# Selective scan: sums issued ahead of the fill of their turn, and the projection's matmuls moved into the turns with sums

## The chip, the cores and the metric

One core of a Trainium2 chip runs the whole program. The metric is device time in microseconds (us) of one execution. Engines: PE (TensorE, matmuls), DVE (VectorE), ACT (ScalarE), POOL (GpSimd), SP (SyncE, which issues the DMAs here). Each works through its own queue in order, and they meet at semaphores.

## The reference, cut to what matters

The model has two layers on four images of 64 x 64 tokens with 128 channels: attention and a recurrent network, then a selective scan in four directions and a mixture of experts. The change lies in the selective scan of the second layer:

```python
x_dbl = einsum('bkdl,kcd->bkcl', xs, x_proj_w)          # x projection: dt's rank 8, B 16, C 16
dts_r, Bs, Cs = x_dbl[:, :, :R], x_dbl[:, :, R:R+N], x_dbl[:, :, R+N:]
dt = softplus(einsum('bkrl,kdr->bkdl', dts_r, dt_proj_w) + dt_proj_b)
A = -exp(A_logs)
def step(h, inp):                                         # over the L = 4096 tokens
    dt_l, u_l, B_l, C_l = inp
    h = h * exp(dt_l[..., None] * A) + (dt_l * u_l)[..., None] * B_l[:, :, None, :]
    return h, einsum('bkdn,bkn->bkd', h, C_l)
ys = ys + Ds * xs                                         # and the four directions are added up
```

There are 4 images, K = 4 directions, 256 channels and N = 16 states for each channel, all in float32.

## The kernel before, in words

The function `scans` (from line 966) handles one direction k after the other, in the order 2, 3, 0, 1. A direction is cut into 33 **windows** of W = 500 tokens (4 blocks of 125), so there are 132 windows. A window has 16 **tiles**: for four states at a time (q = 0 to 3) and each of the four blocks. A tile holds 128 partitions x (2 channel halves x 4 states x 127 columns) = 1016 columns. Tiles of two neighbouring groups q alternate.

The order of all work is written by hand (`tc.manual_schedule()`): a loop over **turns** p issues the instructions of each turn to the engines' queues. A window takes 16 turns, and from here on turns are counted modulo 16, so that "turn 8" is p = 8, 24, 40 and so on. In the kernel before, the order of a turn p is:

- `finished(p)`: once a window, at turn 9, ACT copies the finished `y` from PSUM (L1337), and SP stores it.
- `at[p+1].fill()`: PE fills one of the two `db` PSUM buffers of the tile of turn p+1, with 8 small matmuls (L1241) for dt*u*B. The buffer was read by the scan of turn p-1. Beside each pair a matmul of zeros (L1250) adds nothing to `y`. This is called **F(p+1)** below.
- `at[p-1].carry()`: ACT copies the last states of the tile of turn p-1 into the decays of a later tile (L1286).
- `at[p].scan()`: DVE runs the scan (L1265), called **scan(p)**, which needs F(p) and its decays.
- `sums(p)`: at every even turn, 16 matmuls on 64 x 64 corners of the array (named by L1316 in the profile) add products of a group into `y`: **S(p)**. At turn 7, `add_other` (L1327, **add**) adds what an earlier direction left, or the skip term; not for k = 3.
- `at[p].times_c()`: POOL multiplies the states by C into `products` (L1299), a ring of 12 tiles. It may overwrite a place only when the sums have read it.
- `at[p+5].load()` (SP loads C rows), `before(p)` (SP loads `other`), `decay(p)` (ACT exponentials, L1206).
- `projections(p)`: the generator `project` prepares a later window in steps. `yield t` means: go on at turn t, counted from the window's own start, so -33 falls on turn 15 of the windows under way, and -15 on turn 1.

The steps of `project` that the text speaks of, all sharing the two PSUM banks of one tile, `mm = ps.tile([P, ND, CH], ...)`, made once:

- two x matmuls (L1110), **x1** and **x2**, into `mm[:, 0]`, and the ACT copy `xd` (L1115) out of it;
- the dt matmuls (L1129), **dt**, into both banks, then on ACT `e`, `low`, a logarithm back into `mm`, on POOL a product into `low` (L1145);
- two DVE maxima (L1154), **dt0** and **dt1**, which read bank 0 and bank 1 of `mm` at turns 13 and 14;
- POOL's `dtu` (L1157); the small transposes of B (L1162), **b_ps**, into `mm[:, 1]`; two DVE products `b_diag` (L1168) that read them at turns 2 and 3;
- ACT copies `quarters` (L1177), eight transposes (L1189), **T**, into both banks of `mm`, and the ACT copy `dtu_t` (L1191).

Of the kernel before, what the change touches and what calls it, by code (L numbers as in the profile page):

```python
# [965 lines left out]
def scans(ctx, tc, a, us, ys, flag):  # L966
# [19 lines left out]
    TILES = Q * NB  # L986
# [100 lines left out]
    def quartered(of, to, turned):  # L1087

        for half in range(2) if turned else (None,):
            i = NB if half is None else NB // 2  # L1090
            yield (
                to if half is None else to[:, :, 2 * half : 2 * half + 2],
                bass.AP(
                    of.tensor,
                    of.offset + (0 if half is None else (2 - 2 * half) * T),
                    [of.ap[0], [STEP, NS], [T, i], [1, 32]],
                ),
            )

    def project(v):  # L1100

        k = v.k
        yield -BEFORE
        v.u = work.tile([P, ND, W], F32, tag="u", name="u")
        for b, of, to in v.pieces:
            nc.sync.dma_start(v.u[:, :, to], us[b][k % 2][:, :, of])
        x_ps = mm[:, 0]
        for h, turn in enumerate((-33, -31)):
            yield turn
            nc.tensor.matmul(  # L1110
                x_ps[:, :W], w_x[:, h, k, :], v.u[:, h, :], start=h == 0, stop=h == ND - 1
            )
        yield -30
        xd = work.tile([P, W], F32, tag="xd", name="xd", bufs=1)
        nc.scalar.activation(xd, x_ps[:, :W], AF.Identity, bias=one)  # L1115
        v.c_rows = dram.tile([NB, N, T], F32, tag="c", name="c_rows")
        nc.sync.dma_start(
            v.c_rows.rearrange("i n t -> n i t"),
            xd[64 : 64 + N].rearrange("n (i t) -> n i t", i=NB),
        )  # L1120
        yield -29
        b_rows = work.tile([32 + N, NS, NB, 32], F32, tag="b_rows", name="b_rows", bufs=1)
        for to, of in quartered(xd[32 : 32 + N], b_rows[32:], False):
            nc.scalar.copy(to, of)
        yield -23
        pts = mm[:, :, :W]
        for h, row in enumerate(DT_ROWS):
            rows = slice(row, row + R + 1)
            nc.tensor.matmul(pts[:, h], w_dt[rows, k, :], xd[rows], start=True, stop=True)  # L1129
        yield -22  # L1130
        e = work.tile([P, ND, W], F32, tag="e", name="e", bufs=1)
        if v is todo[0]:

            nc.scalar.preload_act_table_set("natural_log_exp_and_others")
        if flag is None:
            nc.scalar.activation(e, pts, AF.Relu, scale=-1.0, bias=most)
            nc.scalar.activation(e, e, AF.Exp, scale=-1.0, bias=most)
        else:
            nth = todo.index(v)
            nc.scalar.activation(e, pts, AF.Exp, accum_out=largest[:, nth : nth + 1])  # L1140
        low = work.tile([P, ND * NS * P], F32, tag="low", name="low", bufs=1)
        bound = low[:, : ND * W].rearrange("p (h t) -> p h t", h=ND)
        nc.scalar.activation(bound, e, AF.Copy, scale=-0.5, bias=1.0)
        yield -21
        nc.gpsimd.tensor_mul(bound, bound, e)  # L1145
        if flag is None:
            for h in range(ND):
                nc.vector.tensor_max(bound[:, h], pts[:, h], bound[:, h])
        nc.scalar.activation(pts, e, AF.Ln, bias=1.0)
        yield -19  # L1150
        v.dt = work.tile([P, ND, W], F32, tag="dt", name="dt")
        for h, turn in enumerate((-19, -18)):
            yield turn
            nc.vector.tensor_max(v.dt[:, h], pts[:, h], bound[:, h])  # L1154
        yield -17
        dtu = work.tile([P, ND, W], F32, tag="e", name="dtu", bufs=1)
        nc.gpsimd.tensor_mul(dtu, v.dt, v.u)  # L1157
        yield -15
        b_ps = mm[:, 1, : NS * N].rearrange("p (s n) -> p s n", s=NS)
        for i in range(NS):  # L1160
            part = b_rows[32 : 32 + N, i].rearrange("n i t -> n (i t)")
            nc.tensor.transpose(b_ps[:, i, :], part, ident[32 : 32 + N, 32 : 32 + N])  # L1162
        yield -14
        v.b_diag = work.tile([P, NS, N, 32], F32, tag="b_diag", name="b_diag")
        quarters = work.tile([P, ND, NS, NB, 32], F32, tag="low", name="quarters", bufs=1)
        for turn, i in ((-14, 0), (-13, 2)):
            yield turn
            nc.vector.tensor_mul(  # L1168
                v.b_diag[:, i : i + 2].rearrange("p s n t -> p (s n) t"),
                b_ps[:, i : i + 2]  # L1170
                .rearrange("p s (n o) -> p (s n) o", o=1)
                .to_broadcast([P, 2 * N, 32]),
                ident32.rearrange("p (o t) -> p o t", o=1).to_broadcast([P, 2 * N, 32]),
            )
            h = i // 2
            for to, of in quartered(dtu[:, h], quarters[:, h], h):
                nc.scalar.copy(to, of)  # L1177
        yield -12
        v.b_other = work.tile([P, NS, N, 32], F32, tag="b_other", name="b_other")
        for r in range(2):  # L1180
            to, of = (slice(HALF * x, HALF * x + HALF) for x in (r, 1 - r))
            nc.sync.dma_start(v.b_other[to], v.b_diag[of])
        yield -11
        v.dtu = work.tile([P, ND, NS, P], F32, tag="dtu_t", name="dtu_t")
        turned = mm.rearrange("p h (s d) -> p h s d", s=NS)
        for h in range(ND):
            for i in range(NS):
                part = quarters[:, h, i].rearrange("p i t -> p (i t)")
                nc.tensor.transpose(turned[:, h, i, :], part, ident)  # L1189
        yield -10  # L1190
        nc.scalar.copy(v.dtu, turned)  # L1191
# [111 lines left out]
    def sum_of(pair, n):  # L1303

        v, q = pair[0].v, pair[0].q
        if q == 0 and n == 0:
            v.y = ps.tile([P, 2, CH], F32, tag="y", name="y", bufs=1)
            summed.append(v.y)
        for r in range(2):
            rows = slice(HALF * r, HALF * r + HALF)  # L1310
            for h, g in enumerate(pair):
                y = v.y[HALF * h : HALF * h + HALF, r, :W]
                begins = q == 0 and n == 0
                ends = q == Q - 1 and n == 3
                of, to = window_of(products, rows, g, n, v.data.start, y)
                nc.tensor.matmul(to, ident[rows, rows], of, start=begins, stop=ends)  # L1316
        if n == 3:
            summed.append(v.y if q < Q - 1 else None)

    def add_other(v):  # L1320

        if v.k == 3:
            return
        for r in range(2):
            rows = slice(HALF * r, HALF * r + HALF)
            for h in range(ND):
                nc.tensor.matmul(  # L1327
                    v.y[HALF * h : HALF * h + HALF, r, :W],
                    skips[rows, h, :] if v.back else ident[rows, rows],
                    v.other[rows, h, :],  # L1330
                    start=False,
                    stop=False,
                )
# [22 lines left out]
    with tc.manual_schedule():  # L1356
# [58 lines left out]
        def sums(p):  # L1415

            g, turn = divmod(p - 10, NB)
            for g, n in ((g, 0), (g, 1)) if turn == 0 else ((g, 2), (g, 3)) if turn == 2 else ():
                if g in range(len(pairs)):
                    sum_of(pairs[g], n)  # L1420
            w, turn = divmod(p - 23, TILES)
            if turn == 0 and w in range(len(todo)):
                add_other(todo[w])

        def finished(p):
            w, turn = divmod(p - 25, TILES)
            if turn == 0 and w in range(len(todo)):
                finish(todo[w])

        for p in range(-BEFORE, max(at) + 12):  # L1430
            finished(p)
            if p + 1 in at:
                at[p + 1].fill()
            if p - 1 in at:
                at[p - 1].carry()
            if p in at:
                at[p].scan()
            sums(p)
            if p in at:
                at[p].times_c()  # L1440
            if p + 5 in at:
                at[p + 5].load()
            before(p)
            decay(p)
            projections(p)
# [380 lines left out]
```

## Time and profile before

| | |
|---|---|
| median of 3 runs | 9569.09 us (9560.02 to 9577.49) |
| profiled execution | 9570.26 us, span 9568.5 us |
| scans, turns in full flow | about 3640 to 8905 us of the span |
| scan on DVE (L1265) | 2112 times, 2256 ns each |
| products on POOL (L1299) | 2112 times, 2149 ns each |
| matmuls of F (L1241) | 33792, 270 ns median, several at a time on strips of the array |
| matmuls of S (L1316) | 16896, 577 ns median, several at a time on corners of the array |

The span is what the hardware profiler recorded from the first to the last instruction; the execution's own time is a little longer. In an answer of the timeline a row has its start, its length (of several instructions run together where it says x2 and so on), the engine, the line, the tiles and shapes, and in brackets how long the engine had been idle before it and what ended that. Busy time by stage gives stretch, length and busy us (count) for PE, PE's weight loads, DVE, ACT and POOL, then PE's granted clock, the DMA share and GB/s.

### The profile page before, as it was taken

The page shows a single profiled execution, that of the slowest core. Times are in us where ns is not written, and L with a number is a line of the kernel's source. Part 1 is how long each engine was busy: PE and PEld are TensorE (multiplying, and loading weights), DVE is VectorE, ACT ScalarE, POOL GpSimd, SP SyncE. Part 2 cuts the span into 40 slices and gives each one's busy share as a digit, 9 for nine tenths or more (in the row PEclk, how much of TensorE's full clock was granted, in tenths as well). Part 3 has the DMA queues.
Part 4 walks back from the last instruction along what each step waited for, and adds up shares of the span by engine and source line. Part 5 has one row for each costly group of instructions (what it writes and reads, how often), then busy time and mean ns, then how long its engine had stood idle before and what let it go on. Part 6 is the DMA issues. An engine that isn't in the chain of part 4 may idle for free. (4 is left out here: it accounts for less than half of the span.)

```text
span 9568.5 us, 222640 instructions
## 1 busy us (share of the span) xinstructions
PE 8704.4 (91%) x94770; PEld 4134.2 (43%) x94770; DVE 8357.7 (87%) x5099; ACT 6855.5 (72%) x10362; POOL 5157.0 (54%) x2433
## 2 busy tenths in 40 slices
PE   7999999999989887999999999999999999999766
PEld 3222222222223334555555555555555555555223
DVE  6899999999978317999999999999999999999764
ACT  3888888888856456777778788877777777777321
POOL 0000000000001017999999999999999999999100
PEclk8999999999999898999999999999999999999887
DMA  4000000000011335666666666666666666666634
GB/s 174 27 8 36 8 8 34 8 8 8 10 51 53 115 122 155 170 171 170 170 168 160 163 160 160 161 167 170 170 171 171 170 170 171 170 170 164 225 119 181
DMA packets 530898, 1163.76 MB, mean 122 GB/s; under 512 B 76818, under 2 KB 444506, under 8 KB 502106
## 3 DMA queue, kind: packets, MB, share of 16 engines
q1 hardware_dynamic: 529882, 1149.30, 41.4%
q8 instruction: 748, 12.26, 0.5%
q14 instruction: 268, 2.20, 0.1%
HBM read 828.51 MB, written 182.15 MB: 106 GB/s over the span
## 5 line engine op out<-in xcount | busy, mean ns | idle before, releaser
L1265 DVE TENSOR_TENSOR_SCAN states<-decays,db 128x1016 f32<-128x1016 f32 x2112 | 4668.8, 2256 | 100.8 <-ACT decays L1286 60.9
L1299 POOL TENSOR_TENSOR products<-states,c_ring 128x1000 f32<-128x1000 f32 x2112 | 4456.2, 2149 | 219.4 <-PE y L1316 185.3
L1206 ACT ACTIVATE decays<-dt,a_logs 128x500 f32<-128x500 f32 x4224 | 3017.6, 714 | 90.4 <-DVE states L1265 4.3
L1241 PEld LDWEIGHTS db<-b_diag,dtu_t 32*128 32x128 f32 x16896 | 2050.9, 187 | 1607.1 <-DVE states L1265 1187.3
L1241 PE MATMUL db<-b_diag,dtu_t 32*128 32x128 f32 x16896 | 2429.4, 283 | 315.2 <-DVE states L1265 309.5
L1241 PE MATMUL db<-b_other,dtu_t 32*128 32x128 f32 x16896 | 2458.3, 284 | 0.0
L1250 PE MATMUL y<-zeros 32*128 32x128 f32 x14720 | 2122.0, 283 | 0.0
L1241 PEld LDWEIGHTS db<-b_other,dtu_t 32*128 32x128 f32 x16896 | 2049.7, 186 | 0.2 <-issue 0.2
L1316 PE MATMUL y<-products,ident 64*64 64x500 f32 x16896 | 2019.7, 592 | 1.2 <-POOL products L1299 1.2
L334 DVE TENSOR_TENSOR total<-total,ring 128x2048 f32<-128x2048 f32 x768 | 1759.1, 2291 | 67.7 <-DVE total L334 2.7
L1250 PEld LDWEIGHTS y<-zeros 32*128 32x128 f32 x14720 | 1771.8, 186 | 0.0
masks.py:197 POOL MEMSET ident<- 128x128 f32 x6 | 1.2, 204 | 2974.3 <-SPq L180 2677.7
L302 ACT ACTIVATE ring<-sa 128x2048 f32<-128x2048 f32 x640 | 1203.9, 1881 | 454.2 <-PE sa L287 454.2
L311 PE MATMUL av<-ring,v_at 128*32 128x512 f32 x8192 | 1010.0, 599 | 0.1
L1316 PEld LDWEIGHTS y<-products,ident 64*64 64x64 f32 x16896 | 541.2, 132 | 696.7 <-issue 568.1
L287 PE MATMUL sa<-q_at,k_at 32*128 32x512 f32 x5120 | 731.8, 641 | 63.3 <-ACT ring L302 41.6
L1286 ACT COPY decays<-states 128x8 f32<-128x8 f32 x2048 | 405.2, 198 | 535.7 <-DVE states L1265 519.4
L302 ACT ACTIVATE ring<-sb 128x1536 f32<-128x1536 f32 x512 | 741.2, 1448 | 0.4 <-PE sb L287 0.4
L287 PE MATMUL sb<-q_at,k_at 32*128 32x512 f32 x3072 | 555.7, 615 | 50.9 <-ACT ring L302 50.9
L311 PEld LDWEIGHTS av<-ring,v_at 128*32 128x32 f32 x8192 | 210.4, 109 | 701.2 <-issue 676.6
L287 PEld LDWEIGHTS sa<-q_at,k_at 32*128 32x128 f32 x5120 | 200.3, 183 | 618.5 <-ACT ring L302 310.2
L330 DVE TENSOR_TENSOR total<-ring 128x2048 f32<-128x2048 f32 x128 | 293.2, 2290 | 141.4 <-ACT ring L302 141.4
(210 smaller groups left out, 7962.9 us busy)
## 6 DMA issues: line engine op xcount, KB each, us to landing
c_ring<-c_rows SPq DMA_DIRECT2D x2112, 250.0 KB, 4.6
b_other<-b_diag SPq DMA_DIRECT2D x264, 512.0 KB, 6.5
weights<-in_w SPq DMA_DIRECT2D x32, 1024.0 KB, 12.8
u<-u_r SPq DMA_DIRECT2D x60, 500.0 KB, 5.7
y_r<-sum SPq DMA_DIRECT2D x60, 500.0 KB, 4.3
u<-u_c SPq DMA_DIRECT2D x60, 500.0 KB, 5.7
y_c<-sum SPq DMA_DIRECT2D x60, 500.0 KB, 4.1
x<-x SPq DMA_DIRECT2D x96, 256.0 KB, 2.6
```

The costliest lines, as they stand in the source:

```text
L287: nc.tensor.matmul(s[:, m, :], k[rows, tokens(t)], q[rows, chunk(chunk_state["c"])], start=True, stop=True,)
L302: nc.scalar.activation(ring[:, lo : lo + n, :], s[:, at : at + n, :], AF.Exp)
L311: nc.tensor.matmul(chunk_state["av"][rows, :], chunk_state["v"][:, t, rows], ring[:, at + i, :], start=t == 0, stop=t == NJ - 1,)
L330: nc.vector.tensor_add(total, chunk_state["first"], w)
L334: nc.vector.tensor_add(total, total, w)
L1206: nc.scalar.activation(to, dt, AF.Exp, scale=scale)
L1241: nc.tensor.matmul(bank.rearrange("p (n t) -> p n t", n=4)[:, :, to : to + 32], v.dtu[rows, h, s, :], b[rows, s, 4 * self.q : 4 * self.q + ...
L1250: nc.tensor.matmul(y[:, idle // 2, :P], zeros[rows], zeros[rows], start=False, stop=False)
L1265: nc.vector.tensor_tensor_scan(order(self.slot(states)), order(self.slot(decays, shift)), order(self.db[:, SKIP + shift :][:, : 2 * LANE]) ...
L1286: nc.scalar.copy(self.edge(later.slot(decays), later.v.into), last)
L1299: nc.gpsimd.tensor_mul(to, h, c)
L1316: nc.tensor.matmul(to, ident[rows, rows], of, start=begins, stop=ends)
```

## The change

`sums` moves to the front of the turn, ahead of `fill`. `add_other` is split off into `others`, stays behind the fill, and runs one turn earlier (turn 6). The steps of `project` that issue matmuls move from odd to even turns, each by one turn ahead: x1 from -33 to -34, x2 from -31 to -32, dt from -23 to -24, b_ps from -15 to -16, and T from -11 to -12, by leaving out its own `yield`.

```diff
-        for h, turn in enumerate((-33, -31)):
+        for h, turn in enumerate((-34, -32)):
             yield turn
             nc.tensor.matmul(
                 x_ps[:, :W], w_x[:, h, k, :], v.u[:, h, :], start=h == 0, stop=h == ND - 1
             )
...
-        yield -23
+        yield -24
         pts = mm[:, :, :W]
...
-        yield -15
+        yield -16
         b_ps = mm[:, 1, : NS * N].rearrange("p (s n) -> p s n", s=NS)
...
             nc.sync.dma_start(v.b_other[to], v.b_diag[of])
-        yield -11
         v.dtu = work.tile([P, ND, NS, P], F32, tag="dtu_t", name="dtu_t")
...
                     sum_of(pairs[g], n)
-            w, turn = divmod(p - 23, TILES)
+
+        def others(p):
+            w, turn = divmod(p - 22, TILES)
             if turn == 0 and w in range(len(todo)):
                 add_other(todo[w])
...
             finished(p)
+            sums(p)
             if p + 1 in at:
                 at[p + 1].fill()
             if p - 1 in at:
                 at[p - 1].carry()
             if p in at:
                 at[p].scan()
-            sums(p)
+            others(p)
             if p in at:
                 at[p].times_c()
```

## The prediction

> **What bounds the kernel now.** I read the page's busy shares first, then busy time by stage. The scans run from about 3640 to 8905 us; there VectorE (DVE), PE and GpSimd (POOL) are all nearly full:
>
> ```profile
> PE 8704.4 (91%) x94770; PEld 4134.2 (43%) x94770; DVE 8357.7 (87%) x5099; ACT 6855.5 (72%) x10362; POOL 5157.0 (54%) x2433
> 3640.00:8905.00 5265.00, 4944.20 (x68803) 2909.09 (x68803) 5088.69 (x2639) 4128.41 (x7771) 5038.43 (x2374) 1.00 0.62 167
> ```
>
> DVE is busy 97% of the stage, POOL 96%, PE 94%. So a window (16 turns) must be read turn by turn. The timeline of DVE in one window (start, us, then what it waited for in brackets):
>
> ```profile
> 7006.48 4.47 DVE L1265 TENSOR_TENSOR_SCAN states<-decays,db 128x1016 f32<-128x1016 f32 x2 [0.62 <-ACT decays L1286]
> 7011.12 4.43 DVE L1265 TENSOR_TENSOR_SCAN states<-decays,db 128x1016 f32<-128x1016 f32 x2 [0.17 <-PE db L1241]
> 7016.05 0.68 DVE L1154 TENSOR_TENSOR dt<-mm,low 128x500 f32<-128x500 f32 x1 [0.50 <-POOL low L1145]
> 7016.65 2.26 DVE L1265 TENSOR_TENSOR_SCAN states<-decays,db 128x1016 f32<-128x1016 f32 x1
> 7018.82 0.65 DVE L1154 TENSOR_TENSOR dt<-mm,low 128x500 f32<-128x500 f32 x1
> 7019.39 8.83 DVE L1265 TENSOR_TENSOR_SCAN states<-decays,db 128x1016 f32<-128x1016 f32 x4
> ```
>
> DVE loses 0.62 + 0.17 + 0.50 = 1.29 us in this window; by the waits of DVE it recurs in nearly every window that adds the other direction (99 of 132; the interval between two `low` rows is 39.87). In the 33 windows of k = 3 the first wait is absent and the interval is 39.2. Without waits a window is about 38.5. All three waits go back to the late sums of turn 8, S8: the ACT copy of y waits for them, the carry queues behind it; F10 stands behind them on PE; and POOL waits for them, so `low` is late:
>
> ```profile
> 7005.34 8.41 POOL L1299 TENSOR_TENSOR products<-states,c_ring 128x1000 f32<-128x1000 f32 x4 [1.67 <-PE y L1316]
> ```
>
> The part that the change touches next is the first x matmul, x1, on PE:
>
> ```profile
> 7018.96 0.37 PE L1241 MATMUL db<-b_diag,dtu_t 32*128 32x128 f32 x1 [0.35 <-DVE states L1265]
> 7020.06 1.10 PE L1110 MATMUL mm<-u,w_x 128*128 128x500 f32 x2
> 7021.71 0.37 PE L1241 MATMUL db<-b_diag,dtu_t 32*128 32x128 f32 x1 [0.54 <-DVE states L1265]
> ```
>
> x1 runs at 7020.06, just after the second dt maximum, dt1, ended (7018.82 + 0.65 = 7019.47). That is no accident of the data: in the built program x1 waits for dt1, in both kernels, though x1 writes bank 0 of `mm` and dt1 reads bank 1. Two lines, of the view of L1110 and of the waits (us in total, times, longest), show that the two banks are tied: x1 once really waited; xd, reading bank 0, waits each window for b_diag, reading bank 1:
>
> ```profile
> DVE dt L1154: 6.1, 1
> ...
> ACT xd L1115 <- DVE b_diag L1168: 272.4, 131, 3.0
> ```
>
> [...] F1, whose scan was done, came only after x1. So what stands behind a waiting x1 is late with it. [...]
>
> **The change, part by part.** No instruction is added or removed, and the orders on ACT, DVE, POOL and SP are unchanged. All cost is in PE's order, per window:
> - before: F15 S14 | F0 x1 | F1 S0 | F2 b_ps x2 | F3 S2 | F4 | F5 S4 | F6 T | F7 S6 | F8 add | F9 S8 | F10 dt | F11 S10 | F12 | F13 S12 | F14
> - after: S14 F15 x1 | F0 | S0 F1 b_ps x2 | F2 | S2 F3 | F4 | S4 F5 T | F6 | S6 F7 add | F8 | S8 F9 dt | F10 | S10 F11 | F12 | S12 F13 | F14
>
> Steps on PE, start to next start, from this window's rows: F 1.10; S 1.84; x 1.04; b_ps 0.29; T 1.07; add 1.00; dt 0.62. F(p) starts 0.11 after the DVE instruction that follows scan(p-2); scan(p) starts 1.30 after a late F(p) (7009.82 to 7011.12). DVE: scan to next 2.19, dt0 0.60, dt1 0.57, the two b_diag 1.14 and 1.11. As a test, walking the old order with these gives 39.88 against 39.87 measured.
>
> Now the new order, time 0 at the start of scan(13), first without a wait for `low`:
> - F14 0.11, S14 1.21, F15 3.05. PE would reach **x1** at 4.15, but dt1 (behind dt0 and scan(14)) starts at 4.96 and ends at 5.61: x1 starts at 5.67. Before, F0 with its own wait filled this gap.
> - F0 6.71, so scan(0) at 8.01, not 7.72: **+0.29**. S0 7.81, F1 9.65: scan(1) 10.95, not 10.21: **+0.74**. b_ps 10.64, x2 10.93, F2 11.97: scan(2) 13.27, not 13.15: **+0.12**.
> - The two b_diag now give PE time: F4 16.01, S4 17.11, F5 18.95, T 20.05 (it gains an explicit wait for the second b_diag, which ends at 19.98), F6 22.19, waiting for DVE. No loss. T costs nothing because F6 would wait until 22.19 anyway; the cover is 1.07.
> - S6 23.29, F7 25.13, add 26.23, F8 27.23, S8 28.33, F9 30.17: scan(9) 31.47, not 30.84: **+0.63**. dt, F10 31.89 (in time), S10 32.99, F11 34.83: scan(11) 36.13, not 35.87: **+0.26**.
> - S8 ends at 30.24, before scan(8) does (30.9): POOL's 1.67 and ACT's 1.48 are gone. POOL then follows DVE: scan(11) ends 38.37, its product 40.5, `low` 42.85; dt0 would stand at 42.71, so **+0.18** in place of 0.50.
>
> Delays: 0.29 + 0.74 + 0.12 + 0.63 + 0.26 + 0.18 = 2.22. Those of before cost 1.29 as shown and about 0.05 more each, since scans without a wait overlap by that: 1.4. The interval of the walk is 40.70 in place of 39.88, **+0.82**. For k = 3 (no add) F8 and F9 come 0.66 earlier, the 0.63 is gone and 0.25 is left at scan(11): 40.04 in place of 39.22, again +0.82. Sum: 132 x 0.82 = **+108 us**. Costed at nothing: the sums' own inputs (S14 needs the product of turn 11, done at 40.6 - 40.5 = 0.1, S14 stands at 1.2; S6 has 1.9 to spare; a late S14 would hide in front of x1), the u load (issued at turn 8, 5.7 us to landing), the add's loads (turn 13, used nine turns later), and the dt matmul one turn earlier (mm is free since turn 6). Not shown by the trace: how x1 resumes after a wait. A matmul row that follows a wait (F) takes 0.37 where others take 0.27, so up to 0.1 more, once per window (+13 us); at the other end nothing, or a little gain where DVE is freer than walked. I take 0.
>
> The profiled execution took 9570.26 us (span 9568.5), 1.2 above the median 9569.09. 9570.3 + 108 = 9678; from the median 9677. I say 9678.
>
> **Rivals.**
> - *x1 doesn't wait.* If only bank 0 counted, x1 would need dt0 alone and start at 4.15; F0 5.19, F1 8.13, F2 10.45: no scan late there. Left are 0.63, 0.26 and 0.18: 39.53 and, for k = 3, 38.87, both 0.35 less than before: -46 us, **9524**. It decides if x1 starts before about 4.9. For it: the gain at S8 is real. Against: the written wait and the 272.4 us above. 0.12.
> - *They balance*: x1 starts at about 5.2, and its loss eats the 0.35: **9570**. Nothing in the profile puts x1 there. 0.03.
> - *Same mechanism, dearer*: in the windows at a lower clock (0.83 between 3400 and 3640) and on resuming PE is slower, adding 0.1 to 0.3 per window to the four late fills: up to 9718. Within the range.
>
> **How the numbers follow.** The main case has 0.85 with its own range 9635 to 9725 (each of the five PE terms may be off by 0.05 to 0.1, hence 30 to 45 us). To allow for a smaller x1 loss the range begins at 9615. A measurement here can tell about 0.2%, 19 us, from no change. Slower 0.85, same 0.03, faster 0.12.
>
> **What would show it.** Right: x1 [idle <- DVE dt] of about 1.5 us in each window; scans waiting for PE db in turns 0, 1, 9 and 11, about 2.0 us a window; POOL no longer waiting for PE y; dt waiting under 0.3 for `low`; `low` rows 40.7 and 40.0 apart. Wrong: x1 within 1.2 us of F15, no scan of turns 0 and 1 waiting, or intervals under 39.9.

## The result: 3.0% slower, and the profile after

The changed kernel takes **9854.36 us** (median of 5 runs, 9844.81 to 9875.27) where the kernel before takes 9569.09: a ratio of 1.0299, with a 95% interval of 1.0285 to 1.0313. That is +285 us, where the prediction said +108. The direction was right, and so was the mechanism it named; two more losses came on top that it had put at nothing.

The page of the kernel after: busy time, share of the span and count by engine; then two rows of its costliest groups (busy time and mean ns of one; after the last bar, the engine's idle time in front of the group, and what ended most of it):

```profile
PE 8757.7 (89%) x94778; PEld 4165.0 (42%) x94778; DVE 8386.1 (85%) x5099; ACT 6862.3 (70%) x10362; POOL 5196.4 (53%) x2433
L1264 DVE TENSOR_TENSOR_SCAN states<-decays,db 128x1016 f32<-128x1016 f32 x2112 | 4692.7, 2258 | 320.3 <-PE db L1240 268.5
L1298 POOL TENSOR_TENSOR products<-states,c_ring 128x1000 f32<-128x1000 f32 x2112 | 4493.4, 2143 | 462.8 <-DVE states L1264 425.1
```

No engine has more to do: a scan still takes 2258 ns, a product 2143. What grew is waiting. The scans stand 320.3 us idle, mostly for F (PE db), and POOL now waits for the scans. Busy time by stage, for the turns in full flow, 5540 us long where it was 5265:

```profile
3640.00:9180.00 5540.00, 4985.61 (x68743) 2936.38 (x68745) 5115.93 (x2638) 4135.72 (x7771) 5072.41 (x2372) 0.97 0.59 158
```

DVE's share is 5115.93 / 5540 = 92%, where it was 97%, and **the third number from the end, PE's granted clock, is 0.97 where it was 1.00.** Now one window of DVE, from one `low` to the next:

```profile
7057.16 0.68 DVE L1154 TENSOR_TENSOR dt<-mm,low 128x500 f32<-128x500 f32 x1 [0.19 <-POOL low L1145]
7057.76 2.26 DVE L1264 TENSOR_TENSOR_SCAN states<-decays,db 128x1016 f32<-128x1016 f32 x1
7059.94 0.65 DVE L1154 TENSOR_TENSOR dt<-mm,low 128x500 f32<-128x500 f32 x1
7060.51 2.26 DVE L1264 TENSOR_TENSOR_SCAN states<-decays,db 128x1016 f32<-128x1016 f32 x1
7063.00 2.27 DVE L1264 TENSOR_TENSOR_SCAN states<-decays,db 128x1016 f32<-128x1016 f32 x1 [0.24 <-ACT decays L1285]
7065.94 4.61 DVE L1264 TENSOR_TENSOR_SCAN states<-decays,db 128x1016 f32<-128x1016 f32 x2 [0.67 <-PE db L1240]
7071.10 1.23 DVE L1168 TENSOR_TENSOR b_diag<-mm,ident 128x1024 f32<-128x1024 f32 x1 [0.55 <-PE db L1240]
7072.23 2.26 DVE L1264 TENSOR_TENSOR_SCAN states<-decays,db 128x1016 f32<-128x1016 f32 x1
...
7087.11 11.14 DVE L1264 TENSOR_TENSOR_SCAN states<-decays,db 128x1016 f32<-128x1016 f32 x5 [0.60 <-PE db L1240]
7098.45 0.68 DVE L1154 TENSOR_TENSOR dt<-mm,low 128x500 f32<-128x500 f32 x1 [0.20 <-POOL low L1145]
```

scan(0) is late by 0.24, scan(1) by 0.67, scan(9) by 0.60, and `low` costs 0.19: close to the 0.29, 0.74, 0.63 and 0.18 of the walk. (The 0.24 is put down to ACT's carry; but F0 started at 7061.70, and 1.30 later is 7063.00, so F0 sets this start too.) The delay of scan(2) has no bracket, but the row of scans 1 and 2 is 4.61 long where two scans took 4.43 to 4.47. The wait that the walk did not have is the **0.55 in front of the first b_diag**. The distance from dt0 to dt0, 98.45 - 57.16 = 41.29 us, is what the walk's 40.70 and about 0.6 give.

PE in the same window, then the F3 matmul for which b_diag waited:

```profile
7060.69 1.08 PE L1110 MATMUL mm<-u,w_x 128*128 128x500 f32 x2 [1.72 <-issue]
7061.70 0.37 PE L1240 MATMUL db<-b_diag,dtu_t 32*128 32x128 f32 x1
7062.79 1.91 PE L1315 MATMUL y<-products,ident 64*64 64x500 f32 x16
...
7070.79 0.27 PE L1240 MATMUL db<-b_diag,dtu_t 32*128 32x128 f32 x1
```

x1 waits 1.72 us and starts as dt1 ends (7059.94 + 0.65 = 7060.59). The view names "issue" as the end of this wait, not DVE, so it is dt1's end that one compares. Over the whole run (us in total, times, longest):

```profile
PE mm L1110 <- issue: 223.1, 129, 1.7
...
DVE b_diag L1168 <- PE db L1240: 70.5, 129, 0.6
```

The third loss is not in every window. In this one x1 was followed by a clock of half speed; PE, then DVE, then busy time by stage (the clock is the third number from the end):

```profile
4333.01 1.99 PE L1110 MATMUL mm<-u,w_x 128*128 128x500 f32 x2 [1.73 <-issue]
4334.93 0.58 PE L1240 MATMUL db<-b_diag,dtu_t 32*128 32x128 f32 x1
4335.30 0.42 PE L1240 MATMUL db<-b_diag,dtu_t 32*128 32x128 f32 x1
```

```profile
4332.83 2.26 DVE L1264 TENSOR_TENSOR_SCAN states<-decays,db 128x1016 f32<-128x1016 f32 x1
4336.94 2.27 DVE L1264 TENSOR_TENSOR_SCAN states<-decays,db 128x1016 f32<-128x1016 f32 x1 [1.86 <-PE db L1240]
```

```profile
4333.00:4335.00 2.00, 1.99 (x5) 0.54 (x5) 2.00 (x1) 0.91 (x2) 2.00 (x2) 0.51 0.37 118
4335.00:4337.00 2.00, 2.00 (x28) 1.81 (x32) 0.14 (x2) 1.82 (x4) 2.00 (x2) 0.64 0.37 118
4338.00:4340.00 2.00, 2.00 (x37) 1.41 (x30) 1.34 (x2) 0.75 (x2) 2.00 (x1) 1.00 0.47 130
```

The pair of x matmuls takes 1.99 instead of 1.08, an F matmul 0.58 and then 0.42 instead of 0.37 and 0.27, and scan(0) waits 1.86 instead of 0.24. Between 3720 us, where the scans are in full flow, and the last dt maximum, the trace's record of the granted clock has 61 such stretches, 242 us in all (3.4 us each, some twice that); in the kernel before it has one. A window with one of 3.4 us is 42.9 us long, 1.6 more.

### The profile page after: what moved, and what is told of

The parts are those of the page before. It is cut to its first block, busy times and chain, and to the rows that moved or that the text cites. A ratio compares the mean times of both kernels' runs of the same rounds, so it can differ in the third digit from the quotient of the medians.

```text
span 9852.6 us, 222657 instructions
## 1 busy us (share of the span) xinstructions
PE 8757.7 (89%) x94778; PEld 4165.0 (42%) x94778; DVE 8386.1 (85%) x5099; ACT 6862.3 (70%) x10362; POOL 5196.4 (53%) x2433
## 5 line engine op out<-in xcount | busy, mean ns | idle before, releaser
L1264 DVE TENSOR_TENSOR_SCAN states<-decays,db 128x1016 f32<-128x1016 f32 x2112 | 4692.7, 2258 | 320.3 <-PE db L1240 268.5
L1240 PE MATMUL db<-b_other,dtu_t 32*128 32x128 f32 x16896 | 2419.7, 286 | 0.0
L1315 PE MATMUL y<-products,ident 64*64 64x500 f32 x16896 | 2074.2, 606 | 2.8 <-POOL products L1298 2.8
L1249 PEld LDWEIGHTS y<-zeros 32*128 32x128 f32 x14728 | 1794.5, 189 | 0.0
L1110 PE MATMUL mm<-u,w_x 128*128 128x500 f32 x528 | 317.1, 685 | 269.4 <-issue 223.1
```

The source lines that it names most:

```text
L1110: nc.tensor.matmul(x_ps[:, :W], w_x[:, h, k, :], v.u[:, h, :], start=h == 0, stop=h == ND - 1)
L1240: nc.tensor.matmul(bank.rearrange("p (n t) -> p n t", n=4)[:, :, to : to + 32], v.dtu[rows, h, s, :], b[rows, s, 4 * self.q : 4 * self.q + ...
L1249: nc.tensor.matmul(y[:, idle // 2, :P], zeros[rows], zeros[rows], start=False, stop=False)
L1264: nc.vector.tensor_tensor_scan(order(self.slot(states)), order(self.slot(decays, shift)), order(self.db[:, SKIP + shift :][:, : 2 * LANE]) ...
```

## The experiments

Theory: three losses. (a) x1 waits for dt1 and F0 and F1 are late with it, (b) S2, issued ahead of F3, makes the first b_diag wait, (c) PE's clock drops after the gap in front of x1. The rivals: that (b) or (c) is only a mark of (a), that the moved sums or the moved projection cost by themselves, or that the move of the sums brings a gain that is hidden. "Half-clock" below is the total of the stretches at clock 0.5 between 3720 us and the last dt maximum of each run; intervals are those from dt0 to dt0 of the next window.

| kernel | median us | ratio to before, 95% interval | half-clock us | interval, k = 0 and 1 |
|---|---|---|---|---|
| before | 9569 | | 3 | 39.9 |
| after | 9854 | 1.0299 (1.0285 to 1.0313) | 242 | 41.28, with a stretch 42.9 |
| x1_back | 9672 | 1.0112 (1.0095 to 1.0129) | 17 | 40.70 |
| s2_behind | 9810 | 1.0254 (1.0237 to 1.0271) | 324 | 40.63, with a stretch 42.2 |
| s2_behind_x1_back | 9574 | 1.0009 (1.0002 to 1.0016) | 0 | 40.04 |
| warm | 9741 | 1.0184 (1.0167 to 1.0201) | 14 | 41.28 |
| sums_alone | 10161 | 1.0616 (1.0598 to 1.0633) | 870 | with a stretch 44.37 |
| proj_alone | 9873 | 1.0315 (1.0298 to 1.0333) | 331 | 41.4, with a stretch 42.4 |
| x1_alone | 9596 | 1.0033 (1.0021 to 1.0046) | 7 | 40.1 |
| split | 9522 | 0.9957 (0.9941 to 0.9974) | 3 | 39.66 |
| split_s2_behind | 9480 | 0.9912 (0.9895 to 0.9928) | 3 | 39.33 |
| add_at_3 | 9491 | 0.9917 (0.9901 to 0.9934) | 0 | 39.2 |
| add_at_3_low | 9420 | 0.9843 (0.9826 to 0.9859) | 0 | 38.57 |

**x1_back**: after, with x1 back at turn 15.

```diff
-        for h, turn in enumerate((-34, -32)):
+        for h, turn in enumerate((-33, -32)):
```

> The changed kernel with x1 alone put back to turn 15 (-33), behind F0. Theory: x1's wait for dt1 costs the changed kernel twice: directly (late F0, F1, F2), and through a PE gap of 1.7 us after which the granted clock is 0.5 for 3.4 us in about 60 of the 132 windows. With x1 behind F0, which waits for scan(14) anyway, the gap shrinks to 0.9 us, the halved stretches go, scan(0) is in time and scan(1) is 0.4 late: intervals near 40.7 (no add: 40.1), with b_diag still 0.6 late, so about 9690. Rival 1 (the halved clock has another cause than the gap): the 60 stretches stay, about 9780. Rival 2 (x1 doesn't matter, the sums' place does): unchanged, 9850.

**s2_behind**: after, with the sums of turn 2 alone behind the fill.

```diff
-            sums(p)
+            if p % TILES != 2:
+                sums(p)
             if p + 1 in at:
                 at[p + 1].fill()
+            if p % TILES == 2:
+                sums(p)
```

> The changed kernel with the sums of turn 2 alone put back behind the fill of their turn (F3 ahead of S2). Theory: the first b_diag overwrites a buffer that F3 is the last to read, so S2 ahead of F3 delays b_diag by about 0.55 us in each window; this goes: b_diag no longer waits for PE db, intervals 40.7 where 41.28 was, so 132 x 0.57 = -75 us, about 9780, with the halved-clock stretches as they are (their number may shift by some ten, +-20 us). Rival: the b_diag wait is only a symptom of a generally late PE, and the delay moves to scan(4) or scan(5): no gain, 9850.

**s2_behind_x1_back**: both edits.

> Both of the two edits: S2 behind F3, and x1 at turn 15. Theory: only the delays at scan(1), scan(2), scan(9), scan(11) and the wait for low are left; intervals near 40.1 with add and 39.5 without, no halved clock in the scans: 9570 + 132 x 0.25 = about 9600. Rival (the edits share one cause): their gains don't add, 9690 or more.

With x1 back, 183 of the 285 us are gone: the interval falls by 0.58 (132 x 0.58 = 77 us), and the half-clock by 225 us (66 lengths of 3.4 us, at 1.6 each 106 us). The wait of b_diag is untouched, so (b) is no mark of (a). DVE's waits in x1_back:

```profile
DVE b_diag L1168 <- PE db L1240: 70.5, 129, 0.6
```

With S2 back that row is gone and the interval is 0.65 shorter, with x1 moved (41.28 to 40.63) and with x1 back (40.70 to 40.04). That is (b): 132 x 0.65 = 86 us. In s2_behind alone only 45 us show, because the half-clock grew from 242 to 324 us: 24 lengths of 3.4 us at 1.6 each give back 38. With both edits 9 us are left of the loss (1.0009), some 25 less than expected. So the rest of the change nearly comes out even; that what is gained at S8 is lost at F9 and F11 is the walk's account, and no run took these apart.

**warm**: after, and six matmuls of zeros into `y`, which add nothing, in front of x1.

```diff
             yield turn
+            if h == 0 and summed[-1] is not None:
+                for _ in range(6):
+                    nc.tensor.matmul(
+                        summed[-1][:, 0, :P], zeros, zeros, start=False, stop=False
+                    )
```

> The changed kernel with six matmuls of zeros (128 x 128 x 128, adding zero to y) on PE in front of x1, at the place where PE idles for 1.7 us; x1 itself still waits for dt1. Theory: the idle gap is what halves PE's granted clock; filled with work, the 60 halved stretches in the scans go and every window has the 41.28 interval (no add: 40.5), so about -90 us, 9765; x1 starts as late as before or by up to 0.2 later if six are too many. Rival (the clock is halved for another reason, such as the load): the stretches stay and the time is 9850 or a little more.

PE has more to do and x1 and all that stands behind it start no earlier, as the base interval of 41.28 shows, yet the kernel is 113 us faster. Busy time by stage:

```profile
3640.00:9065.00 5425.00, 5070.27 (x70276) 3072.28 (x70280) 5115.70 (x2638) 4133.79 (x7769) 5067.60 (x2372) 1.00 0.60 162
```

The clock is back at 1.00 while b_diag still waits 70.4 us. That is (c) by itself, **113 us**; the half-clock fell by 228 us, 67 lengths of 3.4 us, and 67 x 1.6 = 107.

**sums_alone**: before, with only the sums moved (and `add_other` one turn earlier, as in the change); the projection stays.

```diff
-            w, turn = divmod(p - 23, TILES)
+
+        def others(p):
+            w, turn = divmod(p - 22, TILES)
...
+            sums(p)
...
-            sums(p)
+            others(p)
```

> One part alone: the sums ahead of the fill of their turn and the add in turn 6, with all matmuls of the projection left in the odd turns. Theory (walk of PE): projection and sums then stand in one interval between two fills; scans are late by 0.4 (turn 1), 0.7 (b_diag), 1.0 (turn 7), 0.7 (turn 9) and 0.3 (turn 11): intervals near 41.8, +250 us, about 9820 (9760 to 9870), with no halved clock since x1 stands behind F0. Rival (the projection's move is what costs; the sums' move is free or a gain by POOL's and ACT's waits): 9500 to 9570.

A miss: it is the slowest of all. PE's order leaves a longer gap here, in front of F6. PE's and DVE's timeline of one window:

```profile
7030.57 0.57 PE L1241 MATMUL db<-b_diag,dtu_t 32*128 32x128 f32 x1 [2.12 <-DVE states L1265]
```

```profile
7028.26 6.81 DVE L1265 TENSOR_TENSOR_SCAN states<-decays,db 128x1016 f32<-128x1016 f32 x3
7038.69 4.43 DVE L1265 TENSOR_TENSOR_SCAN states<-decays,db 128x1016 f32<-128x1016 f32 x2 [3.62 <-PE y L1250]
```

The F matmul after 2.12 us of idleness takes 0.57, as the one at the halved clock above (0.58), and a scan waits 3.62. The trace has 128 stretches of half clock in the 132 windows, where the 1.72 us of the changed kernel brought 61. That nearly every window pays is what the expectation lacked; b_diag waits here too (71.8 us in 129 windows), though x1 was not moved: (b) comes from the sums.

**proj_alone**: before, with only the projection's steps moved.

```diff
-        for h, turn in enumerate((-33, -31)):
+        for h, turn in enumerate((-34, -32)):
...
-        yield -23
+        yield -24
...
-        yield -15
+        yield -16
...
-        yield -11
```

> The other part alone: the projection's matmuls in even turns, sums and add as in the kernel before. Theory: x1 now stands behind S14 and waits for dt1 about 1.0 us (less than in the changed kernel, so fewer halved stretches or none); scans late by 0.3 (turn 0), 1.0 (turn 2) and 1.25 (turn 10): intervals near 41.3 with add, about 9760 (9700 to 9820). Rival (x1's wait is the whole cause, 0.3 direct): about 9610.

Slower than expected by about 110 us: the base interval is 41.4, but 73 half-clock stretches came on top, behind a PE gap of 1.9 us in front of a fill. So neither half of the change is the good one: the sums alone are slower than both together, the projection alone is no faster.

**x1_alone**: before, with x1 alone one turn earlier.

```diff
-        for h, turn in enumerate((-33, -31)):
+        for h, turn in enumerate((-34, -31)):
```

> The kernel before with x1 alone moved to turn 14 (-34), where it stands behind F15 and S14 and waits for dt1. Theory: x1 waits about 1.0 us there, F0 and scan(0) are 0.3 late and nothing else: +40 us, about 9605; the gap on PE is near 1.0 us as where no halved clock was seen, so few or no halved stretches in the scans. Rival (any wait of x1 for dt1 brings halved stretches as in the changed kernel): 9650 or more.

x1 waits in every window here too, but for 1.0 us:

```profile
PE mm L1110 <- issue: 119.8, 124, 1.0
```

The clock has one stretch, as before, and the cost is 0.2 a window. So waiting as such did not bring the halved clock: 124 waits of at most 1.0 us are in that row.

**split**: after, with `mm` as two tiles of one bank each, so that x1 depends on dt0 alone. The ACT steps that took both banks at once are issued for each (more ACT instructions). **split_s2_behind** has S2 behind its fill too.

```diff
-    mm = ps.tile([P, ND, CH], F32, tag="mm", name="mm", bufs=1)
+    mm = [ps.tile([P, CH], F32, tag=f"mm{h}", name=f"mm{h}", bufs=1) for h in range(ND)]
...
-        x_ps = mm[:, 0]
+        x_ps = mm[0]
...
-        nc.scalar.activation(pts, e, AF.Ln, bias=1.0)
+        for h in range(ND):
+            nc.scalar.activation(pts[h], e[:, h], AF.Ln, bias=1.0)
...
-        nc.scalar.copy(v.dtu, turned)
+        for h in range(ND):
+            nc.scalar.copy(v.dtu[:, h], turned[h])
```

> The changed kernel with mm made as two tiles of one bank each, so that x1 (bank 0) depends on dt0 alone and no longer on dt1; the ACT steps over both banks (exponential, logarithm, dtu_t) become two instructions each, some 1.4 us more ACT work a window. Theory: x1 starts right behind F15, no scan is late in turns 0 to 2 by it, no gap and no halved clock; b_diag's wait (0.55) stays: the walk gives 39.53 + 0.6 with add and 38.87 + 0.6 without, about 9590 (to 9640 if the longer ACT steps make a carry late). Rival (the wait in front of x1 is of no account beside the sums' place): 9800 or more.

> The same with the sums of turn 2 behind F3. Theory: both missing waits gone, 39.53 and 38.87 as in the prediction's rival in which x1 does not wait, about 9520 (to 9570 if a carry is late on ACT): the order of the change without its two stalls is a little faster than before. Rival (the order is slower in itself): 9600 or more.

The same order of matmuls that lost 3.0% gains 0.43% once the two banks are untied; better than expected by 68 us. In the turns in full flow ACT is busy 4158.13 us where it was 4135.72 in the changed kernel: 0.2 us more a window, not the 1.4 expected. The row of waits `PE mm L1110 <- issue` is gone. So is ACT's wait of xd for b_diag, which took 259.0 us of before from 3720 to 8700 us: the wait that the prediction had read came from the shared tile, and split frees xd together with x1. DVE in one window:

```profile
7014.50 8.74 DVE L1271 TENSOR_TENSOR_SCAN states<-decays,db 128x1016 f32<-128x1016 f32 x4
7023.47 1.23 DVE L1174 TENSOR_TENSOR b_diag<-mm,ident 128x1024 f32<-128x1024 f32 x1 [0.22 <-PE db L1247]
```

Scans 15, 0, 1 and 2 run on without a wait, and b_diag waits 0.22, not 0.55, which is 132 x 0.33 = 44 us of that. The rest I can't place. With S2 behind the fill that wait goes too, and 42 us more are saved: 9480, 40 better than expected.

**add_at_3** and **add_at_3_low**: not the change, but its aim, S8 free of the work in front of it, by other means. The kernel before, with `add_other` at turn 3; the second has also POOL's product into `low` issued earlier.

```diff
-            w, turn = divmod(p - 23, TILES)
+            w, turn = divmod(p - 19, TILES)
```

```diff
-        yield -21
...
+        yield -21
```

(In the second diff the `yield` goes from ahead of the product, L1145, to behind it.)

> The kernel before with only the add moved from turn 7 to turn 3, where PE waits for DVE. Theory: of the 1.29 us that DVE waits in a window of before, the 0.62 in front of scan(10) comes from the add ahead of F9, S8 and F10; it goes and the windows with add take 39.2 as those without: 99 x 0.66 = -65 us, about 9500. Rival (S8's lateness doesn't come from the add, or the add at turn 3 makes F4 to F6 late): 9570 or more.

> The same, and POOL's product into low issued one turn earlier, ahead of the product of turn 11 (its inputs are there since 7010.65, POOL is free at 11.6 in the window shown). Theory: dt0 no longer waits 0.5 for low; 132 x 0.5 = -66 us more, about 9435, intervals 38.7. Rival (POOL, at 38.3 us of work a window, becomes the bound, or the sums of turn 14 wait for the product of turn 11): half of it or nothing, 9470 to 9500.

Both came as expected. Moving `add` takes away 0.7 us a window, early `low` 0.6 more; 1.6% faster than before, **add_at_3_low is the fastest of all**. DVE in one window, where dt0 has no wait for `low` left:

```profile
7007.31 0.65 DVE L1154 TENSOR_TENSOR dt<-mm,low 128x500 f32<-128x500 f32 x1
7007.88 2.26 DVE L1265 TENSOR_TENSOR_SCAN states<-decays,db 128x1016 f32<-128x1016 f32 x1
```

## Why the prediction was wrong in size

The ledger, by experiment: 9569 + 172 (warm, where 14 us of half-clock are left) + 113 (the clock) = 9854. Of the 172, b_diag is 132 x 0.65 = 86, which leaves 86 for what the prediction had at 108. The intervals of s2_behind without a stretch say the same: 0.76 a window above before for k = 0 and 1 (40.63 against 39.87), 0.63 for k = 3 (39.83 against 39.20) and 0.49 for k = 2 (40.39 against 39.90), 87 us in all, where 0.82 was walked for each. So the term that was walked came out a fifth too dear, which hid a little of what was left out.

- **x1 waits for dt1: right.** 1.72 us in each of 129 windows, where 5.67 - 4.15 = 1.52 was said. The late scans came in the places named, with 0.24, 0.67, 0.60 and 0.19 for 0.29, 0.74, 0.63 and 0.18; scan(2) and scan(11) show only as rows 0.1 to 0.2 longer.
- **POOL and ACT are rid of S8: right.** POOL's wait for y (PE y), the 185.3 us of before, is down to 1.6 in the turns in full flow. No net gain is left of it: s2_behind_x1_back stands at 1.0009.
- **"The two b_diag now give PE time ... No loss": the first step that failed.** It looked at what b_diag gives to PE, and took b_diag to start right behind scan(2). b_diag is itself written into a buffer which F3 is the last to read, and F3 now stands behind S2. The trace of before showed that there was nothing to spare, though no wait: F3's last matmul of `b_diag`, and what DVE did next:

```profile
7027.85 0.27 PE L1241 MATMUL db<-b_diag,dtu_t 32*128 32x128 f32 x1
7028.16 1.22 DVE L1168 TENSOR_TENSOR b_diag<-mm,ident 128x1024 f32<-128x1024 f32 x1
```

  The last one ended at 7028.12, and b_diag started 0.04 later, the same 0.04 as in the window after (7070.79 + 0.27 = 7071.06; 7071.10). The walk had F2 at 11.97, so S2 at 13.07 and F3 at 14.91. In the rows above, F3's last matmul of `b_diag` ends 1.15 after F3's first started (at 7026.97), and b_diag follows 0.04 later, so b_diag could not start before 16.10, where scan(2) leaves DVE free at 15.46: a line for this wait would have given 0.64, beside the 0.65 that s2_behind measured.
- **"How x1 resumes after a wait ... I take 0": the second, and the larger.** The bounds were 0 and 0.1 us a window. The 13 us of the upper end stand against 113: not a resume cost of a matmul, but 61 stretches of 3.4 us or more at half the clock. (Nor is a row of 0.37 the mark of a wait: F3's first row in before, at 7026.97, takes 0.37 with no wait in front of it.) The text named a lower clock only as a reason why PE might be slower in stages that had it already, not as something that the new gap could bring on. The gaps that recur in the trace of before are 0.6 us at most, but one fill came after 1.73 us of idleness, and the price stands right behind it; PE, busy time by stage, DVE:

```profile
6274.01 0.37 PE L1241 MATMUL db<-b_diag,dtu_t 32*128 32x128 f32 x1 [1.73 <-DVE db L1233]
6274.90:6278.30 3.40, 3.40 (x25) 0.96 (x19) 3.33 (x2) 2.24 (x5) 3.40 (x2) 0.50 1.01 262
6279.89 4.43 DVE L1265 TENSOR_TENSOR_SCAN states<-decays,db 128x1016 f32<-128x1016 f32 x2 [1.65 <-PE db L1241]
```

  One gap, 3.4 us at clock 0.50, and a scan 1.65 late: had a gap of 1.5 us in each window been priced by these rows, the upper end would have been, as an estimate, 132 x 1.65 = 218 us, not 13.
- **A reading that does not hold:** the row of F1 in before does not show that PE keeps to its order, since F1 itself waits 0.54 there for scan(15). The rows of the changed kernel show it: scan(14) ended at 7060.02, yet F0 started at 7061.70, behind x1.
- **The rival "x1 doesn't wait"**, with 9524, did not happen here, but its arithmetic can be read off split: 9522. In part that is chance: split still has 0.22 at b_diag, which the rival's sum did not, and 38.54 and 39.33 in split_s2_behind are 0.2 to 0.3 below its 38.87 and 39.53.

## What to carry to other kernels

When a step on an in-order engine moves later, walk not only who reads its result but who may overwrite its inputs: a buffer whose writer starts 0.04 us after its last reader was as good as a wait here, though the view of waits showed none. The tile over two PSUM banks tied together steps that share no bank (x1 waited 1.72 us for dt1); splitting it turned this change from +3.0% to -0.4%. And price a new recurring gap on PE with the clock: look in the recorded clock of the kernel before for what followed a gap of that length, even if there is only one; if the clock fell, either shorten the gap (x1_back, 183 us with the late fills) or fill it, for even useless matmuls paid here (113 us).

## What was not expected of the hardware

The longest gap that recurs on PE against the stretches of half clock, in 132 windows: 0.6 us (before), 1; 1.0 to 1.1 (x1_alone, s2_behind_x1_back, x1_back, warm, split), 0 to 3; 1.7 (after, s2_behind), 61 and 64; 1.9 (proj_alone), 73; 2.1 (sums_alone), 128. So gaps of 1.72 us brought 61 stretches in 132 windows, and gaps of 1.0 to 1.1 us at most 3.

Which windows pay can be read off the traces. In those of before and after all changes of the recorded clock (129 and 308) lie on a grid of 3.413 us, to within 0.001 us. Cut the time from 3720 us to the last dt maximum into the cells of that grid, and add up PE's idle time in each cell that runs at full clock. In the changed kernel 62 cells have 1.56 us of idleness or more (a value fitted to the traces), and behind 60 of them the clock is halved in the next cell; of the other 1442, with less, 1 is followed so. In the kernel before it is the only cell above 1.56 us (1.73), and none of the other 1490. A gap of 1.72 us thus counted when it fell into one cell nearly whole, and not when an edge of the grid cut it. In sums_alone the interval is 44.37 us in all four directions, with and without add: 13 steps of the grid. So the gap would meet the grid at nearly the same place in every window, and 128 stretches in 132 windows fit that. No run moved a gap within the grid and left all else as it was, so this fits the traces, but no experiment has tested it.
